# Two conditional expert bodies moved ahead of the 26 expert blocks, with buffers of their own

## The chip, the cores and the metric

The kernel runs on one core of a Trainium2 chip. A core has five engines that run side by side and meet through semaphores: PE (TensorE, matmuls), DVE (VectorE), ACT (ScalarE), POOL (GpSimd) and SP (SyncE, which here only issues transfers). Transfers are carried by 16 DMA engines and are issued from SP's queue, and, where rows are gathered by an index, from POOL's. The metric is the device time of one execution in microseconds; the median of three runs of the kernel before is 453.46 us.

## The reference, cut to what matters

There are 2048 tokens (8 batches of 256) of 256 features. Four layers follow each other: a cross-attention, a mixture of experts, a second cross-attention, and an 8-bit linear layer. The change lies in the second of them:

```python
logits = einsum('btd,ed->bte', x, gate_w) + expert_bias       # 8 experts and 4 "zero" experts
topk_logits, topk_idx = top_k(logits, 2)
topk_w = softmax(topk_logits)
h = silu(einsum('btd,efd->btef', x, w1))                      # per expert: 256 -> 512
y = einsum('btef,edf->bted', h, w2)                           # per expert: 512 -> 256
out = einsum('bte,bted->btd', w_ffn, y) + w_zero[..., None] * x
```

Each token uses two experts of twelve; a zero expert hands the token back. So the number of rows that each expert sees is known only when the routing is computed.

## The kernel before, in words

After the first attention the kernel routes. It writes the normalised tokens to two places in memory, `rows` (where the experts read them) and the tail of `made` (where a zero expert's answer is read). It counts the tokens of each expert, rounds each count up to whole blocks of 128 rows, and lays the blocks of all experts one behind the other. `which_i[j]` is then the expert of block j, `from_i[:, j]` the 128 token numbers of block j, and `blocks_i` the number of blocks that are filled.

`NB` = 39 blocks is the most that any routing can need. The kernel always computes the first `NU0` = 26. Blocks 26 to 29 stand in a first conditional body, blocks 30 to 38 in a second; a body is skipped when `blocks_i` says that no block of it is filled. With the inputs of this case neither body runs.

A block j consists of these steps:

- `fetch(j)`, POOL: gathers 128 rows of 256 words from `rows` into one of `NX` = 4 buffers `xb`.
- `load_w1(j)`, SP: reads `which_i[j]` into a register and loads that expert's w1 (512 KB) into one of `NW` = 3 buffers.
- `turn_x(j)`: two PE transposes (L972) and a DVE copy `xbT` (L974).
- `hidden(j)`: PE matmuls into a PSUM bank `bh` (L980; eight in the program, 16 in the trace) and ACT's Silu into `hidT` (L985).
- `result(j)`: PE reads `which_i[j]`, multiplies by that expert's w2, which is resident (L991), ACT copies `by` to `yb` (L997), and SP stores `yb` into `made` (L998).

The order inside a body is written out by hand (`blocks`, L1000): the transposes of block j+1 stand between `hidden(j)` and `result(j-1)`; `load_w1` runs three blocks ahead and `fetch` four. Small pieces of other work are threaded in by the dictionary `beside`: most of them DVE work (`spread`) that prepares keys for the second attention.

Each engine runs its own list of instructions, in order. A conditional body becomes, on each of the five engines, a read of `blocks_i` (L1028), a compare-and-branch (L1030 for the first body, L1032 for the second), the body, and a short stretch for the case that the body is skipped. In that stretch each queue waits until its semaphores have the values that they have ahead of the body, and then adds what the body would have added: SP does so in nine steps (its own counter and eight counters of transfers, so it waits there for the transfers under way), PE in two, DVE and ACT in one each, and POOL in waits followed by one instruction that counts up the counters of its own transfers. The instructions behind a body wait for counts that include it.

Behind the bodies the second attention begins: `fetch_back` (L1081, POOL) gathers for each token its two answers from `made`, DVE adds them to the residual `x` (L1095), the norm follows (L1060 to L1073), then PE's transposes (L1109), the query projection (L1118), and the loop over the steps of attention. POOL's first `fetch_back` and DVE's first instruction there (clearing `mpad`, L1270) wait for every transfer counter.

## Time and profile before

| What | Value |
|---|---|
| median of three runs | 453.46 us (452.87 to 453.68) |
| the profiled execution's own time | 452.69 us |
| its span, first to last instruction | 451.0 us |
| mean granted PE clock | 0.876 |
| PE, DVE, ACT, POOL busy | 333.4, 231.2, 163.8, 117.2 us |
| first to last L980 matmul of the expert blocks | starts 89.1 to 185.2 us |
| one `fetch` on POOL, median | 997 ns, landing 4.0 us after issue |
| one `load_w1`, median | landing 3.7 us after issue |
| one store of `yb` | landing 1.7 / 2.3 / 3.9 us after issue (min, median, max) |
| last `yb` copy ends | 189.42 us |
| first `fetch_back` on POOL starts | 195.32 us |
| first PE instruction of the second attention | 210.82 us |

Times are microseconds from the first instruction of the profiled execution. "PEld" is PE's weight load, which overlaps matmuls; a name with a small q (PEldq, SPq) means the queue of that engine, where reads of registers, branches and semaphore steps are carried out. The granted clock is the share of full speed that PE was given. A wait is written as who waited, for whom, total us, how often, longest.

### The profile page before, as it was taken

The numbers are of one execution on the slowest core, as the hardware profiler recorded it, in microseconds if no ns is written. First come the engines' busy times: TensorE is split into PE (matmuls) and PEld (weight loads), VectorE is DVE, ScalarE is ACT, GpSimd is POOL, SyncE is SP. The second block draws the span as 40 slices with busy tenths as digits, with TensorE's granted clock in tenths as the row PEclk, the third lists the DMA queues.
The fourth block names the chain that finished last, engine by engine and source line by source line (L and its number), as shares of the span: only waits on it lengthen the run. The fifth ranks groups of instructions, "written<-read, shape, count | busy, mean of one in ns | idle before, by whom it ended". The sixth has DMA issues, their size and how long they took to land. (4 is left out here: it accounts for less than half of the span.)

```text
span 451.0 us, 6387 instructions
## 1 busy us (share of the span) xinstructions
PE 333.4 (74%) x2111; PEld 228.9 (51%) x2111; DVE 231.2 (51%) x705; ACT 163.8 (36%) x320; POOL 117.2 (26%) x153
## 2 busy tenths in 40 slices
PE   7897899699999999702865885587567878772173
PEld 4686666389998999601223442343334343441041
DVE  5769998412434222133365356544654346534884
ACT  2475568122223222202214432334225433352483
POOL 4643512422223220054717200602002000000700
PEclk8989899999999999955866998698978989988566
DMA  5892023586666665121211100100000000000013
GB/s 166 253 347 106 2 93 114 170 286 211 212 192 211 202 208 162 49 62 35 81 35 40 54 1 1 35 13 23 0 1 0 2 0 1 1 1 0 0 47 141
DMA packets 26515, 40.14 MB, mean 89 GB/s; under 512 B 4432, under 2 KB 13744, under 8 KB 26480
## 3 DMA queue, kind: packets, MB, share of 16 engines
q1 hardware_dynamic: 22720, 31.94, 21.3%
q0 software_dynamic: 2784, 7.61, 5.7%
q8 instruction: 20, 0.33, 0.3%
q10 hardware_dynamic: 976, 0.14, 0.2%
q14 instruction: 15, 0.12, 0.1%
HBM read 29.98 MB, written 9.70 MB: 88 GB/s over the span
## 5 line engine op out<-in xcount | busy, mean ns | idle before, releaser
L1161 PE MATMUL sc<-kd,qT 64*128 64x480 f32 x128 | 41.6, 727 | 35.0 <-DVE mpad L1168 35.0
L1168 DVE TENSOR_REDUCE mpad<-sc 128x4 f32<-128x480 f32 x64 | 38.9, 651 | 48.7 <-PE sc L1161 48.7
L1206 ACT ACTIVATE es<-st 120x1024 f32<-120x1024 f32 x32 | 31.0, 1021 | 61.3 <-PE st L1199 61.3
L980 PE MATMUL bh<-xbT,w 128*128 128x128 f32 x416 | 50.9, 275 | 3.1 <-DMA w<-in_w1T 2.9
L980 PEld LDWEIGHTS bh<-xbT,w 128*128 128x128 f32 x416 | 50.2, 192 | 5.0 <-issue 2.0
L991 PE MATMUL by<-w,hidT 128*128 x208 | 49.0, 379 | 0.0
L974 DVE COPY xbT<-bx 128x256 f32<-128x256 f32 x26 | 11.0, 424 | 67.0 <-PE bx L972 67.0
L949 POOL DMA_INDIRECT xb<-rows,from_i x26 | 26.8, 1031 | 62.9 <-PE bx L972 55.3
L1081 POOL DMA_INDIRECT y<-made,back x32 | 32.5, 1015 | 35.7 <-SPq L1032 27.0
L991 PEld LDWEIGHTS by<-w,hidT 128*128 128x128 f32 x208 | 37.6, 190 | 4.1
L1161 PEld LDWEIGHTS sc<-kd,qT 64*128 64x128 f32 x128 | 11.5, 211 | 51.2 <-issue 46.7
L985 ACT ACTIVATE hidT<-bh 128x512 f32<-128x512 f32 x26 | 15.5, 597 | 43.0 <-PE bh L980 43.0
L1067 POOL TENSOR_TENSOR rs_d<-ve_d,mhalf 128x4 f32<-128x4 f32 x4 | 4.1, 1016 | 81.5 <-DVE ve_d L1065 81.5
L1199 PE MATMUL st<-qm,kq 32*120 32x256 f32 x256 | 25.2, 524 | 0.0
L1199 PEld LDWEIGHTS st<-qm,kq 32*120 32x120 f32 x256 | 14.9, 241 | 17.7 <-issue 16.0
L1109 PE MATMUL pt<-ident,xn 128*128 128x128 f32 x32 | 6.6, 326 | 23.0 <-ACT xn L1073 21.9
L1067 POOL TENSOR_TENSOR rs_c<-ve_c,mhalf 128x4 f32<-128x4 f32 x4 | 4.2, 1044 | 73.2 <-DVE ve_c L1065 73.2
L997 ACT COPY yb<-by 128x256 f32<-128x256 f32 x26 | 9.7, 372 | 33.5 <-PE by L991 33.5
L1073 ACT ACTIVATE xn<-x,off_c,rs_c 128x256 f32<-128x256 f32 x16 | 8.3, 588 | 34.4 <-DVE off_c L1069 34.4
L1136 PE MATMUL po<-wo,cT 128*128 128x256 f32 x64 | 17.7, 421 | 3.5 <-ACT cT L1253 2.8
L1223 ACT COPY vs<-vo 128x512 f32<-128x512 f32 x16 | 9.3, 580 | 28.7 <-PE vo L1218 28.7
L1095 DVE SCALAR_TENSOR_TENSOR x<-y,share,x 128x256 f32<-128x256 f32 x32 | 15.2, 476 | 6.4 <-DMA y<-made,back 5.8
(271 smaller groups left out, 633.6 us busy)
## 6 DMA issues: line engine op xcount, KB each, us to landing
w<-in_w1T SPq DMA_DIRECT2D x26, 512.0 KB, 3.7
w<-in_w2T SPq DMA_DIRECT2D x8, 512.0 KB, 8.8
made<-yb SPq DMA_DIRECT2D x26, 128.0 KB, 2.3
x<-in_x SPq DMA_DIRECT2D x4, 512.0 KB, 7.8
rows<-xn SPq DMA_DIRECT2D x4, 512.0 KB, 2.8
made<-xn SPq DMA_DIRECT2D x4, 512.0 KB, 3.8
out<-ot SPq DMA_DIRECT2D x4, 256.0 KB, 2.0
out<-ot SPq DMA_DIRECT2D x2, 512.0 KB, 2.8
```

Source lines behind the costliest of these rows:

```text
L949: nc.gpsimd.indirect_dma_start(out=xb[j % NX].bitcast(I32), out_offset=None, in_=rows, in_offset=bass.IndirectOffsetOnAxis(ap=from_i[:, j ...
L974: nc.vector.tensor_copy(xbT[j], pt)
L980: nc.tensor.matmul(ph[:, f, :], w1[j % NW][:, dc, f * P : (f + 1) * P], xbT[j][:, dc, :], start=(dc == 0), stop=(dc == DC - 1),)
L985: nc.scalar.activation(hidT[j], ph, AF.Silu)
L991: nc.tensor.matmul(py, hidT[j][:, f, :], w2[:, bass.ds(e, 1), f * D : (f + 1) * D].rearrange("p o d -> p (o d)"), start=(f == 0), stop=(f ...
L1081: nc.gpsimd.indirect_dma_start(out=y.bitcast(I32), out_offset=None, in_=made, in_offset=bass.IndirectOffsetOnAxis(ap=back_i[:, g * NT + c, ...
L1095: nc.vector.scalar_tensor_tensor(x[:, c, :], back_rows[g, c, k], share[:, g * NT + c, k : k + 1], x[:, c, :], ALU.mult, ALU.add,)
L1136: nc.tensor.matmul(po[:, c, :], cT[:, dc, t * P : (t + 1) * P], wo1[:, dc, :], start=(dc == 0), stop=(dc == DC - 1),)
L1161: nc.tensor.matmul(sc[:, n, : HQ * SK], qTs[g][n * HP : (n + 1) * HP, ec, t * P : (t + 1) * P], kd[n * HP : (n + 1) * HP, b, ec, :, :].rea ...
L1168: nc.vector.tensor_reduce(m[:, :, h, (1 - h) * DK].rearrange("p (n r) -> p n r", n=2), sc[:, :, : HQ * SK].rearrange("p n (r h k) -> p n r ...
L1199: nc.tensor.matmul(st[:SK, r, h, :], kq[rows_, b, ec, h, :], qm[rows_, h, :], start=True, stop=True,)
L1206: nc.scalar.activation(es[:, part], st[:SK, part], AF.Exp, scale=1.0 / math.sqrt(DK))
```

## The change

The two conditional bodies stand ahead of the 26 blocks in the program. The first four fetches and the first three loads of w1 are written ahead of them. The bodies get buffers of their own, of which there is one each: `xb_more`, `w1_more`, and the tags `xbT_more`, `hidT_more`, `yb_more`; their PSUM banks all have the tag `more`. In a body the five steps of a block follow each other without running ahead (`more_blocks`). The 26 blocks no longer issue the first fetches and loads themselves.

```diff
+    xb_more = [ex.tile([P, D], F32, name="xb_more", bufs=1)]
+    w1_more = [ex.tile([P, DC, DFF], F32, name="w1_more", bufs=1)]
+
+    def rows_at(j):
+        return xb[j % NX] if j < NU0 else xb_more[0]
+
+    def w1_at(j):
+        return w1[j % NW] if j < NU0 else w1_more[0]
+
+    def of_block(j, tag, bufs=2):
+
+        return dict(tag=tag, bufs=bufs) if j < NU0 else dict(tag=f"{tag}_more", bufs=1)
...
-    def bank(name, tag, shape=(P, 512)):
+    def bank(name, tag, shape=(P, 512), j=0):
+        if j >= NU0:
+            tag = "more"
         return pe_.tile(list(shape), F32, tag=tag, name=name)
...
-    def blocks(first, last, beside={}):
+    def blocks(beside):
 
         with tc.manual_schedule(engines=ALL | {ET_.SP}):
-            for j in range(first, min(first + NX, last)):
-                fetch(j)
-            for j in range(first, min(first + NW, last)):
-                load_w1(j)
-            turn_x(first)
-            for j in range(first, last + 1):
-                if j < last:
+            turn_x(0)
+            for j in range(NU0 + 1):
+                if j < NU0:
                     hidden(j)
...
+    def more_blocks(first, last):
+
+        with tc.manual_schedule(engines=ALL | {ET_.SP}):
+            for j in range(first, last):
+                fetch(j)
+                load_w1(j)
+                turn_x(j)
+                hidden(j)
+                result(j)
+
+    with tc.manual_schedule(engines=ALL | {ET_.SP}):
+        for j in range(NX):
+            fetch(j)
+        for j in range(NW):
+            load_w1(j)
+
+    filled_blocks = nc.values_load(blocks_i[0:1, 0:1], min_val=0, max_val=NB)
+    NU1 = NU0 + 4
+    with tc.If(filled_blocks > NU0):
+        more_blocks(NU0, NU1)
+    with tc.If(filled_blocks > NU1):
+        more_blocks(NU1, NB)
...
-    blocks(0, NU0, beside)
-
-    filled_blocks = nc.values_load(blocks_i[0:1, 0:1], min_val=0, max_val=NB)
-    NU1 = NU0 + 4
-    with tc.If(filled_blocks > NU0):
-        blocks(NU0, NU1)
-    with tc.If(filled_blocks > NU1):
-        blocks(NU1, NB)
+    blocks(beside)
     moe.close()
```

The builder moves instructions that depend on nothing in a body ahead of the branches, engine by engine. In the built program the branches stand, on PE, behind the matmuls of `hidden(0)` and the transposes of block 1; on DVE behind the copies `xbT` of blocks 0 and 1; on ACT behind the Silu of block 0; on POOL behind six fetches; on SP behind three loads of w1.

More of the change, by code (lines that the diff above doesn't have):

```diff
@@ L941, in flamingo_gated @@
     NX = 4
+    NW = 3
     ex = moe.enter_context(tc.tile_pool(name="ex", bufs=2, side="right", reuse_waits="tile"))
-    NW = 3
     xb = [ex.tile([P, D], F32, name=f"xb_{i}", bufs=1) for i in range(NX)]
     w1 = [ex.tile([P, DC, DFF], F32, name=f"w1_{i}", bufs=1) for i in range(NW)]
+    xb_more = [ex.tile([P, D], F32, name="xb_more", bufs=1)]
[6 more added lines that the diff above has]
+        return dict(tag=tag, bufs=bufs) if j < NU0 else dict(tag=f"{tag}_more", bufs=1)
     def fetch(j):
         nc.gpsimd.indirect_dma_start(
-            out=xb[j % NX].bitcast(I32), out_offset=None, in_=rows,
+            out=rows_at(j).bitcast(I32), out_offset=None, in_=rows,
             in_offset=bass.IndirectOffsetOnAxis(ap=from_i[:, j : j + 1], axis=0),
@@ L957, in load_w1 @@
         nc.sync.dma_start(
-            out=w1[j % NW],
+            out=w1_at(j),
             in_=a["w1T"][bass.ds(e, 1)].rearrange("o (c p) f -> p (o c) f", p=P),
         )
-    def bank(name, tag, shape=(P, 512)):
+    def bank(name, tag, shape=(P, 512), j=0):
+        if j >= NU0:
+            tag = "more"
         return pe_.tile(list(shape), F32, tag=tag, name=name)
@@ L969, in turn_x @@
     def turn_x(j):
-        pt = bank(f"bx_{j}", "bx", (P, DC, P))
+        pt = bank(f"bx_{j}", "bx", (P, DC, P), j)
         for dc in range(DC):
-            nc.tensor.transpose(pt[:, dc, :], xb[j % NX][:, dc * P : (dc + 1) * P], ident)
-        xbT[j] = ex.tile([P, DC, P], F32, tag="xbT", name=f"xbT_{j}")
+            nc.tensor.transpose(pt[:, dc, :], rows_at(j)[:, dc * P : (dc + 1) * P], ident)
+        xbT[j] = ex.tile([P, DC, P], F32, name=f"xbT_{j}", **of_block(j, "xbT"))
         nc.vector.tensor_copy(xbT[j], pt)
     def hidden(j):
-        ph = bank(f"bh_{j}", "bh", (P, FC, P))
+        ph = bank(f"bh_{j}", "bh", (P, FC, P), j)
         for f in range(FC):
@@ L980, in hidden @@
                 nc.tensor.matmul(
-                    ph[:, f, :], w1[j % NW][:, dc, f * P : (f + 1) * P], xbT[j][:, dc, :],
+                    ph[:, f, :], w1_at(j)[:, dc, f * P : (f + 1) * P], xbT[j][:, dc, :],
                     start=(dc == 0), stop=(dc == DC - 1),
                 )
-        hidT[j] = ex.tile([P, FC, P], F32, tag="hidT", name=f"hidT_{j}")
+        hidT[j] = ex.tile([P, FC, P], F32, name=f"hidT_{j}", **of_block(j, "hidT"))
         nc.scalar.activation(hidT[j], ph, AF.Silu)
@@ L988, in result @@
         e = nc.tensor.value_load(which_i[0:1, j : j + 1], min_val=0, max_val=NE - 1)
-        py = bank(f"by_{j}", "by", (P, D))
+        py = bank(f"by_{j}", "by", (P, D), j)
         for f in range(FC):
@@ L995, in result @@
             )
-        yb = ex.tile([P, D], F32, tag="yb", name=f"yb_{j}", bufs=3)
+        yb = ex.tile([P, D], F32, name=f"yb_{j}", **of_block(j, "yb", 3))
         nc.scalar.copy(yb, py)
         nc.sync.dma_start(out=made[j * P : (j + 1) * P, :], in_=yb.bitcast(I32))
-    def blocks(first, last, beside={}):
+    def blocks(beside):
         with tc.manual_schedule(engines=ALL | {ET_.SP}):
-            for j in range(first, min(first + NX, last)):
-                fetch(j)
-            for j in range(first, min(first + NW, last)):
-                load_w1(j)
-            turn_x(first)
-            for j in range(first, last + 1):
-                if j < last:
+            turn_x(0)
+            for j in range(NU0 + 1):
+                if j < NU0:
                     hidden(j)
-                if j + NW < last:
+                if j + NW < NU0:
                     load_w1(j + NW)
-                if j + 1 < last:
+                if j + 1 < NU0:
                     turn_x(j + 1)
-                if j + NX < last:
+                if j + NX < NU0:
                     fetch(j + NX)
-                if j > first:
+                if j > 0:
                     result(j - 1)
```

## The prediction

> **What bounds the kernel now.** I read the table of windows first, then the timeline of PE, the waits, and the two branch lines one by one. The windows cut the expert stage into its start, its 26 blocks, the branches behind them, and the start of the second attention (columns: stretch, its length, then busy us and instructions of PE, weight loads, DVE, ACT, POOL; then granted clock, DMA share, GB/s).

> ```profile
> core 0: us, PE busy (x) PEld busy (x) DVE busy (x) ACT busy (x) POOL busy (x), PEclk, DMA share, GB/s
> ...
> 91.40:92.40 1.00, 0.00 (x0) 0.00 (x0) 0.42 (x1) 0.39 (x1) 0.75 (x1) 1.00 1.09 420
> 92.40:189.00 96.60, 96.32 (x661) 90.01 (x661) 26.75 (x74) 25.48 (x52) 20.63 (x21) 1.00 0.60 192
> 189.00:195.30 6.30, 0.00 (x0) 0.00 (x0) 0.42 (x1) 0.37 (x1) 0.00 (x0) 0.80 0.11 29
> ```

> The reader is to see three things: from 92.4 on PE works 96.32 of 96.60 us at full clock, so the blocks have no slack in which a late start could be made good; before that PE idles 1.00 us only; and from 189.0 to 195.3 no engine works at all. That last hole is where the two branches stand. The waits name it:

> ```profile
> POOL y L1081 <- SPq L1032: 27.0, 1, 27.0
> ...
> DVE mpad L1270 <- SPq L1032: 11.5, 1, 11.5
> ```

> POOL and DVE had long passed the branch themselves; they waited for SP to leave it. The two branch lines (L1030 for the first body, L1032 for the second), answered one after the other, show what each queue did there (durations min/median/max in ns, first and last start):

> ```profile
> L1030 SPq EVENT_SEMAPHORE  x9: 17/17/17, 190.0 to 193.3; - x9
> ...
> L1030 PEldq COMPARE_BRANCH  x1: 387/387/387, 187.1 to 187.1; - x1
> ```

> ```profile
> L1032 SPq EVENT_SEMAPHORE  x9: 17/17/17, 193.8 to 194.4; - x9
> ...
> L1032 PEldq EVENT_SEMAPHORE  x2: 51/51/51, 193.3 to 193.5; - x2
> ...
> L1032 PEldq COMPARE_BRANCH  x1: 3966/3966/3966, 189.3 to 189.3; - x1
> ```

> Neither body runs (26 fetches in all), yet a skipped body is not free. SP waits out its stores in nine semaphore steps per body, and PE's second compare-and-branch takes 3.97 us where POOL, DVE, ACT and SP need 0.045 to 0.056. In this place PE's 3.97 us cost nothing: its next work comes at 210.82. In the new place they stand ahead of block 1, which starts at 92.44:

> ```profile
> 89.14 2.02 PE L980 MATMUL bh<-xbT,w 128*128 128x128 f32 x16 [1.79 <-DMA w<-in_w1T]
> 91.00 0.38 PE L972 MATMUL bx<-ident,xb 128*128 128x128 f32 x2
> 92.44 2.02 PE L980 MATMUL bh<-xbT,w 128*128 128x128 f32 x16 [1.06 <-DMA w<-in_w1T]
> ```

> [...] its packet records have one 16 KB packet of PE's instruction queue at 190.30 to 191.88, inside the 3.97 us, and the next block's at 194.02, 0.7 us after the branch ended. [...] PE's first is 387 and its second 3966, so the fetch is extra. [...] the window 220.1 to 223.5 (1.77 of 3.40 busy) is followed by half clock:

> ```profile
> 220.10:223.50 3.40, 1.77 (x7) 0.67 (x7) 2.14 (x4) 0.66 (x1) 2.76 (x3) 1.00 0.34 100
> 223.50:226.90 3.40, 2.38 (x5) 0.69 (x5) 2.66 (x7) 0.00 (x0) 2.48 (x4) 0.50 0.31 93
> ```

> **Part 1, taken out behind the blocks.** The last block's copy ends at 189.42 and its store is issued at 189.45. It lands 2.3 us later at the median of these 26 stores (1.7 to 3.9), so at 191.75. POOL's first fetch back then starts some 0.3 to 0.7 us later, after its row of semaphore waits (before: 0.9 after SP's last step), say at 192.0, against 195.32 now. Gain 3.3 us. The store of this run has its last of 16 pieces at 193.05 and the others by 191.13; [...] Bounds: 1.5 us (landing stays at 193.05) to 3.7 us. The whole rest of the kernel hangs on that fetch (y landing 2.8 us, DVE, norm, PE at 210.82), so the gain reaches the end whole.

> **Part 2, put in ahead of block 1.** [...] Queued behind them are now, on PE, 25 blocks; on POOL, 20 fetches; on SP, 23 w1 loads and all 26 stores.

> - PE: turn_x(1) ends at 91.38. PE leaves the first body's two semaphore steps when its matmuls are done (189.01 after 188.97 in the trace), so 91.42; two steps of 0.15; 3.97 of branch, to 95.7; two more steps, 0.3. Block 1 could start at 96.1 instead of 92.44: loss 3.7 us. The w1 wait of 1.06 us covers the first part of it and is already taken off. Bounds 0 (target block at hand) to 5 (the packet competes with w1 traffic; instruction packets took 0.9 to 1.6 us in busy and in quiet stretches alike, so I take no surcharge).
> - PE's next block of instructions: [...] The next fetch is sent 0.7 us after the branch, at 96.4; the fetch in the branch needed 2.97 us from its start to PE going on. Block 1 would run a few matmuls and then stand to between 97.6 (packet over) and 99.4. Bounds 0 to 3.3 us; I take 2.6.
> - Clock: PE would be idle from 91.4 to 96 or beyond, so [...] 3.4 to some 5.5 us at half clock. The same 16 L1199 matmuls take 2.07 us at half and 1.14 at full clock, so 45% of this is lost: 1.5 to 2.5, I take 2.0. [...]
> - SP: it waits for w1 of block 2 to land (93.7), then some 1.4 us of steps through both bodies, 0.6 of register work: w1 of block 3 is issued near 95.6 instead of 91.19 and lands near 99.5 (3.7 to landing). PE wants it after two whole blocks, at 103.6 or later. Cost nothing; if PE did not lose its 3.7, it would want it at 99.98, still just covered.
> - POOL: its second body waits for the sixth fetch to land (96.2) and spends 0.7 on a step that counts up its semaphores: free at 97.0. The next fetch needs turn_x(2), not before 98. It is used four blocks on (14.9 us). Nothing. DVE and ACT pass in under 2 us, inside PE's gap. Nothing.
> - result(0) waits on PE for older loads alone; the spare buffers and the PSUM tag "more" belong to bodies that do not run, and turn_x, hidden and result keep their buffers. Nothing.

> **Sum** on the profiled execution, 452.69 us (451.0 span and 1.7 around it): -3.3 + 3.7 + 2.6 + 2.0 = +5.0, 457.7. The median of the three runs shown is 0.77 higher, which would give 458.4; I say 458.0.

> **Rivals.**

> 1. The same without the second instruction stall: -3.3 + 3.7 + 2.0 = +2.4, 455.5 (on the median's scale 455.9). For it: a boundary within ten instructions can be misplaced. Chance 0.22; the forecast itself has 0.51.
> 2. Faster: PE's branch is cheap in its new place, because the instructions it jumps to are there already or the 3.97 us were in truth a wait for the quiet tail. Then the existing 1.06 us hides it, the clock stays up, and the 3.3 us are clear gain: 449.4 to 450.2. Against it stands the packet inside the branch and the bodies, still of about 250 and 550 PE instructions. It decides at the start of block 1: up to 92.44 + 3.3 = 95.7 without a cold clock the kernel gains, later it loses. Chance 0.20.
> 3. A wash: a shorter branch or a warmer clock against a late store, 0.07 within 0.2%, which is about what a measurement of this kernel can tell from no change.
> 4. The change does not do what it says, as if the builder had put the branches elsewhere: the built order shows otherwise.

> So faster 0.20, same 0.07, slower 0.73. The slower cases alone span 455 to 461; the range reaches down to 451.0, into part of the faster case.

> **What would show it.** In the changed profile: no idle stretch waiting for SP's branch line, POOL's first y fetch 2.3 to 4.5 us after the last yb copy instead of 5.9; PE's second branch near 4 us at about 91.7; block 1's first hidden matmul at 96 or later, perhaps broken off after a few; clock 0.5 for one or two windows near 94 to 104; then blocks of 3.73 us as now, all late by 6 to 9 us. Block 1 starting by 93 would prove me wrong, as would a branch of under 0.5 us on PE.

## The result, and the profile after

The changed kernel takes 458.14 us (median of six runs, 454.87 to 460.52), the kernel before beside it 453.25 us (median of six, 449.98 to 453.68). The ratio is 1.0116 [1.0066, 1.0165]: slower by 4.9 us. Medians are of all runs of a kernel, ratios of its fast runs alone, which leaves out runs more than 1.5% above its fastest. The times of one kernel spread widely (over 5.7 us in these six of the changed kernel, over 7.6 to 10 us in the three later sets of 42 to 59 runs of the kernel before, one of 1376 us not counted), so single profiles are compared below from a common point: the DVE cast of L844 that makes the row numbers `from_i`, after which the code up to the first gather back is what the change touches.

In the page, the idle time ahead of the hidden matmuls has a new cause, here before and then after the change (busy us, mean ns of one, then idle time before and what ended most of it):

```profile
L980 PE MATMUL bh<-xbT,w 128*128 128x128 f32 x416 | 50.9, 275 | 3.1 <-DMA w<-in_w1T 2.9
```

```profile
L995 PE MATMUL bh<-xbT,w 128*128 128x128 f32 x416 | 54.1, 287 | 5.5 <-PEq L1053 4.7
```

L995 is the old L980, L1053 the second branch. PE now stands 4.7 us for its own branch. The line of that branch, queue by queue:

```profile
L1053 SPq EVENT_SEMAPHORE  x9: 17/17/17, 94.3 to 94.8; - x9
...
L1053 PEldq COMPARE_BRANCH  x1: 3871/3871/3871, 95.1 to 95.1; - x1
L1053 ACTq COMPARE_BRANCH  x1: 45/45/45, 95.2 to 95.2; - x1
```

PE's branch takes 3.87 us where it took 3.97 behind the blocks, and the other engines' again about 0.05. As in the kernel before, a 16 KB packet of PE's instruction queue was sent within it (96.21 to 97.58). PE's timeline of the start (start, duration, in brackets the idle time before and its releaser):

```profile
89.90 0.41 PE L987 MATMUL bx<-ident,xb 128*128 128x128 f32 x2 [3.89 <-DMA xb<-rows,from_i]
90.89 3.52 PE L995 MATMUL bh<-xbT,w 128*128 128x128 f32 x16 [0.58 <-DVE xbT L989]
94.21 0.59 PE L987 MATMUL bx<-ident,xb 128*128 128x128 f32 x2
99.48 3.75 PE L995 MATMUL bh<-xbT,w 128*128 128x128 f32 x16 [4.68 <-PEq L1053]
103.02 0.64 PE L987 MATMUL bx<-ident,xb 128*128 128x128 f32 x2
103.45 2.60 PE L1006 MATMUL by<-w,hidT 128*128 x8
105.88 1.95 PE L995 MATMUL bh<-xbT,w 128*128 128x128 f32 x16
```

Three things are to be seen. Block 1 starts at 99.48 instead of 92.44, with 4.68 us of idle before it where there were 1.06. From there to block 2, PE is slow but never still: no second stop. And the start was late before any branch: block 0's transposes come at 89.90, after 3.89 us of idle (0.90 before), and its hidden takes 3.52 us instead of 2.02. The first was predicted, the second contradicts the prediction, the third it did not see. The table of windows, with the columns of the prediction's, has the clock at half in two stretches, 91.2 to 94.6 and 99.48 to 104.9. The records of the granted clock put the second at 98.03 to 104.86; in the traces of before and after every stretch of one granted clock, up to the last, which the end of the trace cuts off, lasts 3.41 us or a whole multiple of it; such 3.41 us are called a window of the clock below.

```profile
91.20:94.60 3.40, 3.40 (x18) 3.24 (x16) 0.00 (x0) 0.15 (x1) 0.50 (x1) 0.50 0.72 258
94.60:99.48 4.88, 0.20 (x3) 0.03 (x1) 0.43 (x1) 0.45 (x1) 1.00 (x1) 0.85 0.46 135
99.48:104.90 5.42, 5.42 (x22) 5.15 (x23) 0.77 (x5) 0.60 (x1) 0.97 (x1) 0.50 0.13 25
104.90:199.00 94.10, 93.49 (x641) 87.29 (x639) 25.99 (x69) 25.18 (x52) 19.41 (x20) 1.00 0.58 185
199.00:203.70 4.70, 0.00 (x0) 0.00 (x0) 0.44 (x1) 0.05 (x1) 0.00 (x0) 1.00 0.11 31
```

The cause of the late start stands in POOL's timeline, here of the kernel before and then of the kernel after:

```profile
83.55 1.45 POOL L949 DMA_INDIRECT xb<-rows,from_i  x1 [4.95 <-DVE end L846]
```

```profile
85.21 1.29 POOL L962 DMA_INDIRECT xb<-rows,from_i  x1 [6.64 <-DVE ed L861]
```

The first gather waits for a later DVE instruction. In the built program it used to wait for the row numbers; now it also waits for the reduction of L853, which reads the scratch tile `past`. POOL's semaphore steps at that line, again before and then after, show the new wait as their longest:

```profile
L949 POOLq EVENT_SEMAPHORE  x4: 17/17/43, 80.3 to 91.6; - x4
```

```profile
L962 POOLq EVENT_SEMAPHORE  x3: 17/17/4092, 80.3 to 91.9; - x3
```

The step of 4.09 us ends at 84.36, just behind the reduction (83.84 to 84.32), and the gather follows 0.85 us later. L861, which the timeline names, is only the last DVE instruction to end ahead of it. The spare buffers made the experts' pool larger by 9216 bytes per partition, and the pool grows downwards: `xb_0`, which began at byte 159200 of a partition, begins at 149984, and `past` lies at 150848 to 152096. So `xb_0` lies on the scratch tile now, and its first gather waits for that tile's last reader: it starts 2.19 us after the cast instead of 0.50.

The hole at the end, in the timeline of after (ACT's last copy, SP's last store, POOL's first gather back):

```profile
198.68 0.37 ACT L1012 COPY yb<-by 128x256 f32<-128x256 f32 x1 [1.40 <-PE by L1006]
199.07 0.32 SPq L1013 DMA_DIRECT2D made<-yb  x1
...
203.75 1.00 POOL L1108 DMA_INDIRECT y<-made,back  x1 [25.78 <-DMA made<-yb]
```

It waits for the store now, not for SP's branch, as predicted; but the hole is 4.71 us, not the 2.6 that the predicted gain of 3.3 comes to. The profile also lists every DMA packet with its start and length. By these packet records a 16 KB instruction packet of PE ran from 200.28 to 201.73, and the last nine packets of the store started only from 201.71 on: 15 of its 16 pieces had landed by 200.76, the last at 202.90. In before it is the same: the instruction packet ran from 190.30 to 191.88, the last nine packets of the store started from 191.87 on, and its last piece landed at 193.05. What made them wait is not shown; the records do not name the DMA engine.

### The profile page after: what moved, and what is told of

Its sections match the earlier page's. It is cut to its first block, busy times and chain, and to the rows that moved or that the text cites. A ratio compares the mean times of both kernels' runs of the same rounds, so it can differ in the third digit from the quotient of the medians.

```text
span 455.3 us, 6382 instructions
## 1 busy us (share of the span) xinstructions
PE 333.7 (73%) x2111; PEld 229.8 (50%) x2111; DVE 231.4 (51%) x705; ACT 163.6 (36%) x320; POOL 117.0 (26%) x153
## 5 line engine op out<-in xcount | busy, mean ns | idle before, releaser
L1188 PE MATMUL sc<-kd,qT 64*128 64x480 f32 x128 | 39.7, 698 | 34.9 <-DVE mpad L1195 34.9
L995 PE MATMUL bh<-xbT,w 128*128 128x128 f32 x416 | 54.1, 287 | 5.5 <-PEq L1053 4.7
L995 PEld LDWEIGHTS bh<-xbT,w 128*128 128x128 f32 x416 | 53.2, 202 | 7.6 <-issue 5.0
L1226 PEld LDWEIGHTS st<-qm,kq 32*120 32x120 f32 x256 | 14.3, 230 | 16.1 <-issue 14.6
L1163 PE MATMUL po<-wo,cT 128*128 128x256 f32 x64 | 16.2, 393 | 3.5 <-ACT cT L1280 2.8
## 6 DMA issues: line engine op xcount, KB each, us to landing
out<-ot SPq DMA_DIRECT2D x4, 256.0 KB, 2.0
```

What stands on the lines that cost most here:

```text
L995: nc.tensor.matmul(ph[:, f, :], w1_at(j)[:, dc, f * P : (f + 1) * P], xbT[j][:, dc, :], start=(dc == 0), stop=(dc == DC - 1),)
L1163: nc.tensor.matmul(po[:, c, :], cT[:, dc, t * P : (t + 1) * P], wo1[:, dc, :], start=(dc == 0), stop=(dc == DC - 1),)
L1188: nc.tensor.matmul(sc[:, n, : HQ * SK], qTs[g][n * HP : (n + 1) * HP, ec, t * P : (t + 1) * P], kd[n * HP : (n + 1) * HP, b, ec, :, :].rea ...
L1226: nc.tensor.matmul(st[:SK, r, h, :], kq[rows_, b, ec, h, :], qm[rows_, h, :], start=True, stop=True,)
```

## The experiments

All kernels in one table. Except for "hole", the columns in the middle are starts in us from the cast of L844, in the one profile of each; `hidden(2)` is the start of block 2's hidden matmuls, by which every cost of the start is in. "hole" is from the end of the last `yb` copy to the first gather back.

| kernel | 1st gather | hidden(0) | hidden(2) | hole | gather back | median us | ratio to before |
|---|---|---|---|---|---|---|---|
| before | 0.50 | 6.09 | 13.20 | 5.90 | 112.28 | 453.25 | |
| before_again | 0.50 | 6.66 | 16.21 | 5.59 | 114.97 | 452.77 | 0.9997 [0.9969, 1.0026] |
| after | 2.19 | 7.88 | 22.86 | 4.71 | 120.74 | 458.14 | 1.0116 [1.0066, 1.0165] |
| after_again | 2.19 | 7.86 | 23.69 | 2.58 | 119.44 | 458.86 | 1.0141 [1.0096, 1.0186] |
| order | 0.50 | 6.10 | 20.02 | 2.57 | 115.77 | 458.56 | 1.0105 [1.0048, 1.0162] |
| order_2 | 0.50 | 6.40 | 21.21 | 2.57 | 116.96 | 457.78 | 1.0142 [1.0104, 1.0179] |
| before_moved | 2.18 | 7.78 | 16.04 | 5.45 | 114.67 | 453.64 | 1.0038 [1.0008, 1.0068] |
| short | 2.18 | 8.22 | 16.88 | 2.58 | 112.63 | 454.02 | 1.0016 [0.9985, 1.0047] |
| order_short | 0.50 | 6.20 | 14.98 | 2.57 | 110.73 | 451.28 | 0.9980 [0.9949, 1.0010] |
| behind_none | 0.50 | 6.18 | 14.40 | 2.74 | 110.32 | 451.08 | 0.9966 [0.9940, 0.9992] |
| behind_nested | 0.50 | 6.30 | 13.15 | 2.80 | 109.12 | 451.65 | 0.9979 [0.9948, 1.0010] |
| behind_nested_2 | 0.50 | 6.44 | 14.38 | 2.80 | 110.35 | 451.98 | 0.9990 [0.9966, 1.0014] |
| ahead_nested | 0.50 | 6.05 | 22.51 | 2.57 | 118.24 | 456.94 | 1.0106 [1.0062, 1.0150] |
| ahead_nested_pad | 0.50 | 6.53 | 18.62 | 2.57 | 114.36 | 455.56 | 1.0057 [1.0031, 1.0082] |

**after_again** and **before_again**: no edit.

> The changed kernel once more, unaltered, to have it on the same chip beside the next three. Every theory: some 457 to 459 us, with the first gather at 85.2 us, block 1 at 99.5 us, the first gather back about 203.7 us. If the share of the second attention that runs at half clock depends on where a 3.4 us window of the clock falls, the second attention (first gather back to end) varies between profiles of the same code by up to some 4 us; if the change shortens it, it stays at 251.5 us.

> The kernel before once more, unaltered, for a second profile and the spread. Every theory: from the cast that makes the row numbers (L844) to the first gather back 112.3 us as in the first profile, unless the last store's late piece (behind PE's instruction packet) was chance, then down to 110.4 us; the second attention 251 to 256 us, as in the six profiles of other kernels with the same code there.

458.86 us for the changed kernel. Its block 1 came 16.92 us after the cast (16.46 in the first profile), and the hole was 2.58 us, with PE's packet sent at 203.77, when POOL was already gathering (203.59): the 4.71 was chance. before_again has the long hole again, 5.59 us, and again an instruction packet ran beside the store (196.60 to 197.55, the store issued at 195.40; SP passed that store's counter at 198.72). It also has a cold start: half clock from 94.0 to 100.8, so `hidden(2)` came 3.0 us later than in the first profile of the same program. Of the five profiles with the start of before (before, before_again, behind_none and the two behind_nested) three had a cold stretch there. So the same program starts with a cold clock or without one; that this is a matter of where the clock's windows of 3.41 us fall is the author's estimate. The second attention took 253.9 and 253.7 us here, and 251.5 (after) and 255.7 (before) in the first profiles; over all fourteen profiles, whose code there is the same, 250.9 to 256.3. So the 4.1 us that the second attention seemed to give back in the first pair are not the change's.

**order** and **order_2**: the declarations of the spare buffers move ahead of `xb` and `w1`.

```diff
+    xb_more = [ex.tile([P, D], F32, name="xb_more", bufs=1)]
+    w1_more = [ex.tile([P, DC, DFF], F32, name="w1_more", bufs=1)]
     xb = [ex.tile([P, D], F32, name=f"xb_{i}", bufs=1) for i in range(NX)]
     w1 = [ex.tile([P, DC, DFF], F32, name=f"w1_{i}", bufs=1) for i in range(NW)]
-    xb_more = [ex.tile([P, D], F32, name="xb_more", bufs=1)]
-    w1_more = [ex.tile([P, DC, DFF], F32, name="w1_more", bufs=1)]
```

> The two spare buffers are declared ahead of the others, so xb_0 and xb_1 no longer lie where a reduction's scratch tile stands; nothing else moves. Theory A (the late first gather is a wait for that scratch tile, and the late start cools PE's clock before block 0): the first gather starts at 83.5 us instead of 85.2, block 0's hidden takes 2.0 us instead of 3.5, block 1's transposes end near 91.4 instead of 94.8, and the kernel needs some 3.4 us less than the changed one, about 454 to 455 us. Rival (the start is late because of the order of issue, or the clock falls anyway): the start and the time stay as in the changed kernel.

> The changed kernel with the spare buffers declared ahead, once more, since its first timing (458.56 us) did not show the 3.7 us that its profile showed from the cast of L844 to the first gather back. Theory A with colliding fetches: from that cast to the first gather back 115.3 to 117 us in this profile too (119.4 and 120.7 in the changed kernel), median 455 to 457 us. Rival (the earlier start is lost to a longer branch as a rule): 118 us or more, median near 458.5 us.

The start is that of before again, and the two profiles reach the gather back 115.77 and 116.96 us after the cast, against 120.74 and 119.44: the placement is what delayed the first gather. But the times are 458.56 and 457.78, where 454 to 457 were expected, and their intervals overlap with the changed kernel's: this gain is not shown by these timings. The profiled execution of order shows where 5.0 us at the gather back can go: against the first one of after, it took 2.9 us more ahead of the cast and 4.5 us more in the second attention (256.0 against 251.5), which the edit does not touch. Its branch was also longer:

```profile
L1052 PEldq COMPARE_BRANCH  x1: 5271/5271/5271, 94.6 to 94.6; - x1
```

By the packet records two instruction packets of PE were sent within it, at 95.71 (1.47 us) and at 95.74 (2.78 us). That the second is the branch's own, held up by the first, is the author's reading; the records do not say what a packet is for. In order_2 the branch took 3.87 us.

**before_moved**: the placement alone, in the kernel before.

```diff
     w1 = [ex.tile([P, DC, DFF], F32, name=f"w1_{i}", bufs=1) for i in range(NW)]
+    ex.tile([P, 2304], F32, name="spare", bufs=1)
```

> The kernel before with one unused tile of 9216 bytes per partition in the pool of the experts' buffers, as much as the changed kernel's spare buffers take; bodies stay behind the blocks. xb_0 then lies on the scratch tile as in the changed kernel. Theory A (the placement alone makes the late start): the first gather starts 2.18 us after the cast of L844 instead of 0.50, the first matmul of block 0 at 7.9 instead of 6.1 us, and the kernel is 1.7 to 3.7 us slower than before. Rival (the late start needs the new order of issue): gather at 0.50 and no change.

The gather starts at 2.18 and hidden(0) at 7.78, as theory A has it, and nothing but an unused tile has changed. The time is up by 0.38% [0.08%, 0.68%], 1.7 us, at the lower edge of what was expected: `hidden(2)` is 1.8 us later than the mean of the five undelayed profiles (14.27), three of which have a stretch at half clock there anyway. The two lines on which this rests, of PE's timeline:

```profile
91.34 0.41 PE L973 MATMUL bx<-ident,xb 128*128 128x128 f32 x2 [3.79 <-DMA xb<-rows,from_i]
92.34 3.53 PE L981 MATMUL bh<-xbT,w 128*128 128x128 f32 x16 [0.58 <-DVE xbT L975]
```

**short** and **order_short**: bodies of one and three blocks. Blocks 30 to 38 have no code then.

```diff
-        more_blocks(NU0, NU1)
+        more_blocks(NU0, NU0 + 1)
...
-        more_blocks(NU1, NB)
+        more_blocks(NU0 + 1, NU1)
```

> The changed kernel with conditional bodies of 1 and 3 blocks instead of 4 and 9; blocks 30 to 38, which these inputs don't fill, are left out. Theory B (PE's second compare-and-branch takes 3.9 us because its target lies beyond the instructions at hand): with some 60 and 180 PE instructions to skip instead of 250 and 550 it falls to 0.4 us or less, block 1 starts some 4 us earlier than 99.5 us, the clock may stay up, and the kernel gains 3.5 to 6 us against the changed one: 452 to 454 us. Rival (the second branch waits for something else, a transfer or a semaphore): it stays near 3.9 us and the time near 457 to 458 us.

> Both edits: spare buffers declared ahead, and bodies of 1 and 3 blocks (blocks 30 to 38, not filled by these inputs, left out). If the two causes add: first gather 83.5 us, PE's branches under 1 us together, block 1 near 92.6 us, no cold clock, and the kernel ahead of the one before by what the end gains, 1.2 to 3.3 us: 450 to 452.5 us. If they don't add (one hides the other), 452.5 to 455 us.

In both the second branch jumps over some 190 PE instructions instead of 550 and takes

```profile
L1053 PEldq COMPARE_BRANCH  x1: 225/225/225, 98.3 to 98.3; - x1
```

so the 3.9 us come with the long jump and the instruction packet that is sent within it (none was within before's first branch, 0.39 us over some 250), and neither with a semaphore nor with a transfer of data. In short, block 1 starts 3.4 to 3.9 us earlier after the cast than in the changed kernel, without a cold stretch behind it, and 454.02 us is 4.8 us under after_again. order_short, with 451.28, is in the expected range of the case where the causes add; but its interval reaches to 1.001. Between short and order_short stands the edit of order alone: the first gather comes 1.7 us earlier, the gather back 1.9 us, and the ratio falls from 1.0016 to 0.9980, with intervals that overlap. That is less than it could be, for PE's timeline in order_short has a stop that short lacks:

```profile
94.85 2.02 PE L994 MATMUL bh<-xbT,w 128*128 128x128 f32 x16 [1.03 <-DVEq L1050]
96.71 0.27 PE L986 MATMUL bx<-ident,xb 128*128 128x128 f32 x1
97.39 0.33 PE L986 MATMUL bx<-ident,xb 128*128 128x128 f32 x1 [0.41 <-issue]
98.56 1.97 PE L1005 MATMUL by<-w,hidT 128*128 x8 [0.84 <-issue]
```

PE stops between two transposes of one block, released by "issue", that is by nothing that the profile shows. An instruction packet had been sent at 95.02 and ended at 96.00; PE went on 1.39 us after that. The author takes this for the second stop that was predicted for the changed kernel, here some 40 instructions behind the branch and worth 1.7 us (from hidden(1) to hidden(2) 5.51 us, 3.81 in before).

**behind_none** and **behind_nested**: what the end can give. The first leaves the two conditional bodies out; the second puts one inside the other.

```diff
     with tc.If(filled_blocks > NU0):
         blocks(NU0, NU1)
-    with tc.If(filled_blocks > NU1):
-        blocks(NU1, NB)
+        with tc.If(filled_blocks > NU1):
+            blocks(NU1, NB)
```

> The kernel before without its conditional bodies; blocks 26 to 38, which these inputs don't fill, are left out. It bounds what taking the branches from behind the blocks can give. Theory C (the hole behind the last block is SP's steps through two skipped bodies and a store held up by an instruction packet of PE): from the last yb copy to the first gather back 2.6 us as in the changed kernel instead of 5.9, and the kernel 3.3 us faster than before. Rival (the hole is the landing of the last store, with the branches beside it): 4.7 us or more, gain 1.2 us or less.

> The kernel before with the second conditional body inside the first: where neither runs there is one compare-and-branch per engine and one row of steps instead of two. Theory C: SP's second nine steps (1.1 us from 193.3 to 194.4) go, and PE's fetching branch comes 2.2 us earlier, ahead of the last store: the hole falls from 5.9 us to 2.9 to 4.8 us, gain 1.1 to 3.0 us. Rival (the last store's landing decides alone): hole 5.6 us or more and no gain.

> The kernel with the bodies behind the blocks, the second inside the first, once more, for a narrower interval. Theory C: hole of 2.8 us again between the last yb copy and the first gather back, 449.5 to 451.7 us, 0.998 to 0.993 of before. Rival (the 2.8 us of the first profile was chance): 4.5 us or more and no gain.

Without bodies the hole is 2.74 us, nested 2.80: the rest of the hole came with the second branch behind the first. Of the 3.1 us between before and behind_nested some 1.1 are SP's second row of steps, and the rest is the store: SP passed its last store's counter 1.7 us after issuing it (195.30 after 193.59), in before_again 3.3 us after and in before 3.6. The waits of behind_nested, to be held against the 27.0 and 11.5 us of before:

```profile
POOL y L1081 <- SPq L1030: 23.9, 1, 23.9
DVE mpad L1270 <- SPq L1030: 8.4, 1, 8.4
```

and PE's only branch still takes 3.53 us, but starts ahead of the last store and ends beside it:

```profile
L1030 PEldq COMPARE_BRANCH  x1: 3525/3525/3525, 191.2 to 191.2; - x1
```

The instruction packet within it ran from 192.16 to 193.22 and the last store was issued at 193.59, so it did not meet this store; the last piece of the store ahead of it landed 0.9 us behind its other pieces, at 194.43, but that was before the last store had landed (195.28). In the times, though, less than the hole's 2.8 to 3.1 us arrives: behind_none gains 0.34% [0.08%, 0.60%], 1.5 us, and the nested one 0.21% and 0.10%, with both intervals reaching past no change. The profiles say faster, the timings leave open by how much, and for the nested kernel whether at all. Where the rest goes is not settled. The second attention's length, which moves by 5.4 us between profiles of the same code (250.9 to 256.3), may well cover it.

**ahead_nested**: order with the second body inside the first. **ahead_nested_pad**: the same with two more pairs of transposes at the end of the second body, which does not run.

```diff
     with tc.If(filled_blocks > NU0):
         more_blocks(NU0, NU1)
-    with tc.If(filled_blocks > NU1):
-        more_blocks(NU1, NB)
+        with tc.If(filled_blocks > NU1):
+            more_blocks(NU1, NB)
```

```diff
             for j in range(first, last):
                 fetch(j)
...
                 result(j)
+            for _ in range(pad):        # pad=2 in the second body
+                turn_x(last - 1)
```

> The kernel with the spare buffers declared ahead (bodies ahead of the blocks), and the second body inside the first. Theory B: PE meets one compare-and-branch, which fetches (3.9 to 5.3 us), but its sequencer comes to it while hidden(0) still runs, 1.7 to 2.0 us earlier than to the second branch of before: block 1 starts 10.5 to 12.6 us after the cast of L844 instead of 14.4, the clock falls for a shorter time or not, and the kernel is 2 to 5 us faster than with two branches there, 450 to 455 us. Rival (the branch waits for PE's matmuls or for a second instruction block in any case): block 1 as late as with two branches, 14 us or more, and no gain.

> The kernel with nested bodies ahead of the blocks, with two more transposes pairs (eight PE instructions in the machine's form) at the end of the second body, which does not run: only the place of the code behind it moves. Theory D ([...]): that second stop goes, block 1 starts 12.3 to 13.2 us after the cast of L844 instead of 16.1, and the kernel gains some 3 us, 453 to 454.5 us. Rival (PE's stop after the branch is the branch's own price, or a wait for w1): block 1 stays near 16 us.

ahead_nested went against theory B: its block 1 came 16.08 us after the cast, 1.1 to 1.7 us later than in order. The branch did start early, at 92.21, but took 5.48 us, and it did not end the wait. PE's timeline and the branch's line:

```profile
93.17 0.38 PE L986 MATMUL bx<-ident,xb 128*128 128x128 f32 x2
101.34 3.57 PE L994 MATMUL bh<-xbT,w 128*128 128x128 f32 x16 [7.79 <-issue]
```

```profile
L1050 PEldq EVENT_SEMAPHORE  x2: 51/51/51, 97.7 to 97.9; - x2
...
L1050 PEldq COMPARE_BRANCH  x1: 5479/5479/5479, 92.2 to 92.2; - x1
```

The branch ended at 97.69; PE passed three semaphore steps and one weight load and then stood until 101.34, while the next instruction packet ran from 98.44 to 99.93. Theory D has this stop hang on where the landing, the instruction that the branch jumps to, lies in the program. With the eight unexecuted instructions more, the timeline is

```profile
92.50 0.63 PE L986 MATMUL bx<-ident,xb 128*128 128x128 f32 x2
96.19 2.96 PE L994 MATMUL bh<-xbT,w 128*128 128x128 f32 x16 [3.06 <-PEq L1052]
98.94 0.63 PE L986 MATMUL bx<-ident,xb 128*128 128x128 f32 x2
```

Block 1 follows the branch (which ended at 95.73) at once, 13.16 us after the cast: theory D's number. The gather back comes 3.9 us earlier than in ahead_nested; the time is 455.56, 1.4 us less by the medians and 2.2 by the ratios, where 3 were expected, and the two intervals overlap. So eight unexecuted instructions ahead of the landing decided whether PE stood still behind it, for 3.3 us or not at all.

short, order_short and behind_none leave out blocks that other inputs need. No complete version with the bodies ahead of the blocks beat the kernel before. The nested bodies behind them are the best complete version that was run: about 1 us under before, inside its uncertainty.

## Why the prediction was right, and where it was not

458.0 us was predicted, and 458.14 measured. The bound on PE's branch and its place were right; the sum came out because a missing term and a wrong one were of one size. That part is luck, and so is the agreement to 0.1 us, with timings of one kernel that spread over 5.7 us.

- **The end, -3.3 us: right as a rule.** Holes of 2.57 to 2.58 us in seven of the eight profiles with the bodies ahead, 5.45 to 5.90 in three of before's order: 2.9 to 3.3 us less. In the first profile of after only 1.2, where an instruction packet ran beside the last store (200.28 to 201.73, the store issued at 199.07). The lower bound, 1.5 us, stood for such a store; in after_again, the same program, the packet was sent 3.49 us later (203.77) and the hole was 2.58. Two figures of the prediction need a word: the stretch of 189.0 to 195.3, in which "no engine works at all", still holds ACT's last copy and DVE's first instruction, so the hole proper begins at 189.42; and rival 1's sum on the profiled execution is 455.1, not 455.5.
- **The branch ahead of block 1, +3.7 us: right.** 4.68 us of idle instead of 1.06, 3.62 more. Rival 2, a cheap branch in the new place, is out; short shows what it would have looked like. The upper bound of 5 us, dismissed because packets took no longer in busy stretches, was reached in order, where PE stood 6.08 us. The branch itself took 5.27 us there, and 5.48 and 5.06 in ahead_nested and ahead_nested_pad. In order its packet was slow (2.78 us); in the two nested kernels it was sent late, 2.9 and 2.6 us after the branch began, against 1.0 and 1.6 in the two profiles of the kernel nested behind the blocks. Why it was sent late is not shown.
- **The second instruction stop, +2.6 us: wrong for this kernel.** It rested on the author's estimate of how far behind the landing the next instruction packet is needed, and no stop followed: PE worked through block 1 without a break, with the next packet sent at 99.75, after block 1 had begun. Stops like it are in two other runs (ahead_nested 3.3 us, order_short 1.7). Counting PE's instructions in the built programs, ahead_nested lands on number 1726 and stops at about 1730; order_short lands on 1181 and stops at about 1218 to 1220, some 510 below. By this count the changed kernel lands on 1731, about one past the place where ahead_nested stops, and ahead_nested_pad on 1734, and neither stops there. In the trace of before 1491 instructions of PE, weight loads among them, start in the six intervals between the packets sent at 95.55 and 188.13, about 250 to a packet; by this estimate the two stops lie two packets apart. An estimate wrong by a few instructions cost 2.6 us. Rival 1 had this part.
- **The cold clock, +2.0 us: right, a little small.** hidden(1) and result(0) took 3.75 and 2.60 us instead of 2.02 and 1.89, and block 2 lost 2.59 us more than block 1. Its length was the author's estimate, 3.4 to 5.5 us; in the trace PE worked 0.18 of the 3.41 us from 94.62 on, and the clock was then at half for 6.83 us (98.03 to 104.86). This is the second cold stretch; the first, over hidden(0), belongs to the next term.
- **The spare buffers, "Nothing": wrong.** This is the term that took the second stop's place. They moved `xb_0` onto a scratch tile, so the first gather started 1.7 us later; PE's idle stretch ahead of block 0 grew from 0.9 to 3.9 us (its wait for w1 behind that shrank from 1.8 to nothing, with 0.6 us for `xbT` in its place) and the clock fell in every one of the four profiles with that placement. In the first pair of profiles this is 3.4 us at the end of block 1's transposes (94.80 against 91.38). As before also starts cold in some executions, the mean loss is smaller: 1.8 us by `hidden(2)`, 1.7 us [0.4, 3.1] in the timing of before_moved.
- **SP, POOL, DVE and ACT, nothing: right.** SP issued the w1 of block 3 at 96.37 and POOL was free at 99.45, each later than predicted, yet from block 2 on no block waits: 93.49 us of PE in a stretch of 94.10.

From means of the profiles: by `hidden(2)` the changed kernel has lost 9.0 us (23.28 against 14.27), of which 2.7 go with the placement (order has 20.62) and 6.3 are branch and cold clock; the hole gives back 1.2 to 3.3. That leaves 5.7 to 7.8 us, against 4.9 and 6.4 in the two timings.

## What to carry to other kernels

What a skipped body costs depends on the engine whose branch is long and on what that engine has to do next: here PE's 3.97 us were free in front of a hole, and in front of back-to-back matmuls 3.87 us cost 3.62 of idle, with a cold clock (3.75 us for hidden(1) instead of 2.02) on top. Where a second body is needed only if the first is, try it inside the first, so that the skipped case passes one branch and one row of semaphore steps: behind the blocks this took 2.8 to 3.1 us out of the hole in the profiles, though the timings do not settle what is left of it at the end. And when a pool grows, look at what its first buffers now lie on, before counting new buffers as free: here that cost 1.7 us at the first gather.

## What the hardware showed that was not expected

```profile
195.32:451.00 255.68, 161.00 (x1001) 83.06 (x1001) 133.95 (x308) 90.83 (x137) 58.27 (x56) 0.81 0.08 25
```

```profile
203.75:455.30 251.55, 157.47 (x1001) 81.46 (x1001) 134.13 (x307) 90.77 (x137) 58.28 (x56) 0.82 0.08 26
```

The same 1001 matmuls, 3.5 us less PE time and 4.1 us less in all: a difference of this size between two single profiles of this kernel says nothing of a change.
